# A two-layer relational graph network on one core: groups of 512 nodes summed in PSUM, bases over four chunks at once, no copied rows

## The chip, the cores and the metric

The kernel runs on one core of a Trainium2 chip. The metric is the device time of one execution in microseconds (us), lower is better. Times of the changed kernel are compared with those of the kernel before, run on the same chip.

## The reference: what is computed

There are N = 50,000 nodes with 128 features each and E = 850,000 edges, sorted by their destination. Each edge has a source, a destination and one of 16 relations. 50,000 of the edges are loops (one for each node, the last of its edges), so M = 800,000 others are left. A layer sums the sources' features per destination and relation and multiplies them by the matrix of the relation, which is itself a weighted sum of 8 bases. All is float32.

```python
def _rgcn_layer(h, src, dst, rel, basis, w_comp, loop_w, bias):
    W = jnp.einsum('rb,bio->rio', w_comp, basis)          # 16 x 128 x 128 from 8 bases
    seg = dst.astype(jnp.int32) * N_REL + rel.astype(jnp.int32)
    agg = jax.ops.segment_sum(h[src], seg, num_segments=N_ENT * N_REL)
    agg = agg.reshape(N_ENT, N_REL, -1)
    msg = jnp.einsum('nri,rio->no', agg, W)
    out = msg + h @ loop_w + bias
    return jax.nn.relu(out)
h = _rgcn_layer(x, src, dst, rel, basis1, w_comp1, loop_w1, bias1)
h = _rgcn_layer(h, src, dst, rel, basis2, w_comp2, loop_w2, bias2)
out = layernorm(x + h)
```

## The kernel before

**Chunks.** The 800,000 edges are cut into 6,250 tiles of 128 edges, and ten tiles (K) make a chunk: 625 chunks (C) in each of the two layers. For each tile, GpSimd (POOL) issues one indirect DMA (`gather`, L202), which fetches the 128 source rows of 512 bytes, in layer 1 from x and in layer 2 from H1, the first layer's output in HBM. The tiles go to five buffers `rows`, `g0` to `g4`, used in turn (GATHERS). In chunk c, POOL gathers the tiles of chunk c + 2 (L932 to L935). A gather waits until TensorE (PE) has used the tile that it overwrites, which is of chunk c - 3.

**From edges to slots.** A tile's edges end in at most 12 neighbouring nodes (WN), its slots. VectorE (DVE) writes a matrix `hot` (L871) of 128 edges by 8 bases by 12 slots: the weight that the edge's relation has for the base, at the edge's slot. PE multiplies the gathered tile by it (L964, 96 columns). Five tiles share a PSUM bank `pa`, two of which are used in turn, and ScalarE (ACT) copies each to `aT` in SBUF (L972). Two chunks later `slots` (L730 to L740) multiplies the 120 slots of the chunk by the 8 bases: 8 matmuls of 128 columns into one bank `ps` (L734), which ACT copies to `slots` (L739).

**From slots to nodes.** `masks_of` (L742) makes two matrices on DVE that say which node, of the 128 from the chunk's base on, a slot belongs to: one for the chunk's own slots and one for those of the chunk before. `nodes_of` (L757) multiplies them by the slots (L761) into `pn`, adds the loop part, and takes relu (layer 1) or adds x and normalizes (layer 2). Each chunk writes 128 rows, and neighbouring chunks' rows overlap.

**The loop part.** `from_itself` (L692) takes 128 nodes: a transpose (L209), two matmuls of 512 columns by four bases each (L710), a product with the node's weights (L713), the product with the loop matrix (L722, L723), and a sum over nine parts (L726). The result goes to L in HBM (L727) and is read again at the chunk's base (`loaded`, L879).

**Rows copied by hand.** In two of eight chunks the tenth tile isn't gathered by POOL. `row_by_row` (L789) lets a sequencer read the 128 source addresses into registers (L798) and issue 128 DMAs of one row each (L808): SP's for one of the two chunks and ACT's for the other. These instructions stand in the same queues as SP's other loads and as ACT's copies. There are 308 such tiles in the two layers, 154 on each of the two.

**Order.** The order on PE, POOL, DVE and ACT is the program's order (manual schedule, L853). `beside` (L901) puts the other parts' steps between the ten matmuls of a chunk. An engine works its queue in order; a waiting instruction holds those behind it. In the first layer, the lists of sources and slots for later chunks are made alongside, one step a chunk (`later_rows`, L839); ten times each a scatter to FULL (L378) and one to LREL (L434) stand among POOL's gathers.

Of the kernel before, what the change touches and what calls it, by code (L numbers as in the profile page):

```python
# [39 lines left out]
F32 = mybir.dt.float32  # L40
I32 = mybir.dt.int32
# [21 lines left out]
AHEAD = 4  # L63
# [8 lines left out]
BASES = 8  # L72
BY_HAND = 8
# [8 lines left out]
def tile_rgcn_resnorm(  # L82
# [21 lines left out]
    NG, NT = -(-R // P), -(-N // P)  # L104
# [9 lines left out]
    assert D == P and N >= P and edges.shape[0] == 1 and AT * NR == P and PER * NB * WN <= BANK and AT * PER * NB == WEIGHTS and PER == HALF and S <= P and C >= 4 and M > 0 and RUN - LK // 2 == LIVE and 2 * C <= NG * P and N <= 1 << 16 and E % ROW == 0  # L114
# [10 lines left out]
    ROW_AT = dram.tile([2 * C, P], I32, name="ROW_AT")  # L125
    NL = -(-(N + LK) // P) * P
    LREL = dram.tile([2 * NL, 1], I32, name="LREL")

    L = [dram.tile([N, D], F32, name=f"L{n}") for n in range(2)]
# [67 lines left out]
    ps_o = ctx.enter_context(tc.tile_pool(name="ps_o", bufs=1, space=PSUM))  # L197
    ps_n = ctx.enter_context(tc.tile_pool(name="ps_n", bufs=1, space=PSUM))
    ps_h = ctx.enter_context(tc.tile_pool(name="ps_h", bufs=2, space=PSUM))
# [6 lines left out]
    def turned(h, m, sb):  # L206

        tp = ps_o.tile([P, D], F32, name="po")
        nc.tensor.transpose(tp[:, :m], h, ident[:m, :m])  # L209
        hT = sb.tile([P, P], F32, name="hT")  # L210
        nc.scalar.copy(hT[:, :m], tp[:, :m])
        return hT[:, :m]
# [8 lines left out]
    key = consts.tile([P, 2 * C * HALF], BF16, name="key")  # L221


    base_i = consts.tile([1, C], I32, name="base_i")
    slot = consts.tile([P, C], F32, name="slot")
    next_slot = consts.tile([P, C], F32, name="next_slot")
    last_slot = consts.tile([P, 1], F32, name="last_slot")
    first_of = consts.tile([1, C], F32, name="first_of")
    base1 = consts.tile([1, C], F32, name="base1")
    minus = consts.tile([1, S], F32, name="minus")  # L230
# [4 lines left out]
    picked = consts.tile([P, 5 * NG + len(ROWS) + 4], F32, name="picked")  # L235
    ones = consts.tile([P, max(LIVE, C)], F32, name="ones")
# [10 lines left out]
    nc.vector.memset(minus, -1.0)  # L247
# [5 lines left out]
    def set_up(pool):  # L253
# [14 lines left out]
        po = ps_o.tile([P, D], F32, name="po")  # L268
# [146 lines left out]
    def loops_of(g, pool, m, d_i, k_f, r_i, loop, loops, asked):  # L415
# [15 lines left out]

        nc.vector.tensor_scalar(picked[0:1, 5 * g + 4 : 5 * g + 5], d_i[0:1, 0:1], float(asked()), None, op0=OP.is_ge)
        yield
# [8 lines left out]
    def rows_of(j, pool):  # L442
# [3 lines left out]
        parts = pool.tile([P, 2, LIVE, 2], F32, name="parts")  # L446
        for h in range(2):
            nc.sync.dma_start(
                parts[:m, h],
                FULL[h * NP + r0 * LIVE : h * NP + (r0 + m) * LIVE].rearrange("(p e) w -> p e w", e=LIVE),  # L450
            )
        if j:
            yield
        srcf = pool.tile([P, LIVE], F32, name="srcf")
        nc.vector.tensor_tensor(srcf[:m], parts[:m, 0, :, 0], parts[:m, 1, :, 0], op=OP.add)
        node = pool.tile([P, LIVE], I32, name="node")
        nc.vector.tensor_tensor(node[:m], parts[:m, 0, :, 1], parts[:m, 1, :, 1], op=OP.add)
# [20 lines left out]
        row_at = pool.tile([P, LIVE], F32, name="real").bitcast(I32)[:, :P]  # L478
        nc.vector.tensor_scalar(row_at[:m], srcf[:m, LIVE - P :], float(N - 1), float(4 * D), op0=OP.min, op1=OP.mult)
        nc.sync.dma_start(ROW_AT[r0 : r0 + m], row_at[:m])  # L480

# [3 lines left out]
        keyf = pool.tile([P, LIVE], F32, name="keyf")  # L485
# [6 lines left out]
        if (r0 + m) * LIVE > M:  # L492
# [6 lines left out]
                beyond[:m], place[:m, :LIVE], last[:m], 64.0, op0=OP.subtract, op1=OP.mult  # L499
# [8 lines left out]
        po = ps_o.tile([P, D], F32, name="po")  # L508
# [6 lines left out]
        nc.vector.tensor_scalar(base1[:, c0 : c0 + cs], half[0:1, :, 0], float(N - P), None, op0=OP.min)  # L515
        nc.vector.tensor_scalar(base_i[:, c0 : c0 + cs], base1[:, c0 : c0 + cs], float(4 * D), None, op0=OP.mult)

        a, b = max(c0 - 1, 0), c0 + cs - 1
        off = pool.tile([1, P], F32, name="off")
        nc.vector.tensor_tensor(off[:, : b - a], base1[:, a + 1 : b + 1], base1[:, a:b], op=OP.subtract)  # L520
        yield
        po = ps_o.tile([P, D], F32, name="po")
        for h in range(2):
            nc.tensor.matmul(po[:S, :cs], spread[h], half[:, :, h], start=h == 0, stop=False)
        nc.tensor.matmul(po[:S, :cs], minus, base1[:, c0 : c0 + cs], start=False, stop=True)
        nc.vector.tensor_scalar(slot[:S, c0 : c0 + cs], po[:S, :cs], within[:S], None, op0=OP.add)
        yield
        po = ps_o.tile([P, D], F32, name="po")
        nc.tensor.matmul(po[:, : b - a], ones[0:1, :P], off[:, : b - a], start=True, stop=True)
        nc.vector.tensor_tensor(next_slot[:S, a:b], slot[:S, a:b], po[:S, : b - a], op=OP.subtract)  # L530
        if b == C - 1:
            nc.vector.tensor_tensor(
                last_slot[:S], next_slot[:S, b - 2 : b - 1], po[:S, b - a - 1 : b - a], op=OP.subtract
            )
# [6 lines left out]
            ones[:m, :LIVE],  # L541
# [6 lines left out]
    def count_up(pool):  # L548
        last = 5 * NG + len(ROWS)
        off = pool.tile([1, C], F32, name="off_all")  # L550

        nc.vector.memset(off, float(N - 1))
        nc.vector.tensor_copy(off[:, : C - 1], first_of[:, 1:])
        nc.vector.tensor_tensor(off, off, base1, op=OP.subtract)
        nc.vector.scalar_tensor_tensor(
            off, off, float(P - 1), ones[0:1, :C], op0=OP.is_le, op1=OP.mult, accum_out=picked[0:1, last : last + 1]
        )

        in_time = pool.tile([1, C], F32, name="in_time")
        nc.gpsimd.iota(  # L560
            in_time,
            pattern=[[P * NT // C, C]],
            base=P * AHEAD - P,
# [3 lines left out]
        nc.vector.tensor_tensor(off, base1, in_time, op=OP.subtract)  # L567
        nc.vector.scalar_tensor_tensor(
            off, off, 0.0, ones[0:1, :C], op0=OP.is_le, op1=OP.mult, accum_out=picked[0:1, last + 1 : last + 2]
        )  # L570

        nc.vector.tensor_tensor(off[:, : C - 3], base1[:, 2 : C - 1], first_of[:, 1 : C - 2], op=OP.subtract)
        nc.vector.tensor_tensor(off[:, C - 3 : C - 2], base1[:, C - 1 :], first_of[:, C - 3 : C - 2], op=OP.subtract)
        nc.vector.scalar_tensor_tensor(
            off[:, : C - 2],
            off[:, : C - 2],
            1.0,
            ones[0:1, : C - 2],
            op0=OP.is_ge,
            op1=OP.mult,  # L580
            accum_out=picked[0:1, last + 3 : last + 4],
        )
        nc.vector.tensor_scalar(picked[0:1, last + 2 : last + 3], first_of[:, 0:1], 0.0, None, op0=OP.is_equal)
# [3 lines left out]
        total = ps_o.tile([P, D], F32, name="po")  # L587
# [4 lines left out]
            off[:, 1:2], total[:1, 1:2], float(E + 2 * NG * (P + 1) + 3 * C - 1), None, op0=OP.not_equal  # L592
# [3 lines left out]
    def normed(t, m, sb):  # L596

        *_, o = normed_steps(t, m, sb)
        return o

    def normed_steps(t, m, sb):
        st = sb.tile([P, 6], F32, name="st")
        nc.vector.bn_stats(st[:m], t)  # L603
        mv = sb.tile([P, 2], F32, name="mv")
        nc.vector.bn_aggr(mv[:m], st[:m])
        sd = sb.tile([P, 1], F32, name="sd")
        nc.scalar.activation(sd[:m], mv[:m, 1:2], AF.Sqrt, bias=eps[:m])  # L607
        yield
        rs = sb.tile([P, 1], F32, name="rs")
        nc.vector.reciprocal(rs[:m], sd[:m])  # L610
        nm = sb.tile([P, 1], F32, name="nm")
        nc.vector.scalar_tensor_tensor(nm[:m], mv[:m, 0:1], -1.0, rs[:m], op0=OP.mult, op1=OP.mult)
        o = sb.tile([P, D], F32, name="o")
        nc.scalar.activation(o[:m], t, AF.Identity, bias=nm[:m], scale=rs[:m])  # L614
        yield o

    def chunked():
        with (
# [8 lines left out]
            def at(c):  # L627

                if c % BASES == 0:
                    _, starts[:] = nc.values_load_multi_w_load_instructions(  # L630
                        base_i[0:1, c : min(C, c + BASES)],
                        engines=[mybir.EngineType.SP],
                        min_val=0,
                        max_val=(N - P) * 4 * D,
                        skip_runtime_bounds_check_because="bases are clamped to N - P, and no node is below 0",
                    )
                return starts[c % BASES]

            def nodes_at(of, start):
                return of.bitcast(U8).rearrange("n d -> (n d)")[ds(start, P * 4 * D)].rearrange("(p d) -> p d", p=P)  # L640

            def weights(c, n):
# [14 lines left out]
                for j in range(PER):  # L657
# [6 lines left out]
                    )  # L664
                yield pm.rearrange("e (t b) -> e t b", b=NB)

            def loop_weights(i, n):

                m = min(AT, NT - i) * NR
                rel = hp.tile([P, 2, P], I32, name="lrel")  # L670
# [536 lines left out]
```

## Time and profile before

| | |
|---|---|
| median of 3 runs | 19472.55 us (19454.4 to 19488.24) |
| the profiled execution | 19472.55 us, its span 19470.8 us |
| PE | 11516.4 us busy, 59% |
| POOL | 11559.5 us busy, 59% |
| DVE | 6757.1 us busy, 35% |
| ACT | 2523.1 us busy, 13% |
| TensorE clock granted, mean | 0.722 |
| DMA engines | 2 tenths busy, 63 GB/s |
| first gather of layer 1, of layer 2 | at 46.52 us, at 9864.63 us |

The span is divided by two layers of 625 chunks, so a chunk takes about 15.6 us. No engine is busy for more than 59% of the span: what sets the time must be read from what each engine waits for. In the profile's groups, a float32 matmul is two records, so that 24,384 records of L964 are 12,192 matmuls. "Busy" is the union of an engine's records. "issue" as the end of a wait means that the profile shows nothing that was waited for.

### The profile page before, as it was taken

What the parts mean: (1) busy time and instruction counts of PE and PEld (TensorE: products, weight loads), DVE (VectorE), ACT (ScalarE), POOL (GpSimd) and SP (SyncE); (2) the same over time, 40 slices, a digit from 0 to 9 for tenths busy, and PEclk for the clock granted to TensorE, in tenths of its full rate; (3) what the DMA queues carried; (4) which work ended last, traced back from release to release, by engine and by line L of the source; (5) the groups of instructions that cost most, each with busy time, mean ns of one, the idle gap of its engine ahead of it and who ended that gap; (6) DMA issues with size and microseconds to landing.
All of it is one profiled execution on the core that took longest, in us unless ns stands there. A gap on an engine that the chain in (4) does not pass through costs nothing. (4 is left out here: it accounts for less than half of the span.)

```text
span 19470.8 us, 266458 instructions
## 1 busy us (share of the span) xinstructions
PE 11516.4 (59%) x59202; PEld 9701.4 (50%) x59202; DVE 6757.1 (35%) x14585; ACT 2523.1 (13%) x6567; POOL 11559.5 (59%) x12224
## 2 busy tenths in 40 slices
PE   4555555555566665566655556556656565666666
PEld 3444444454455555555545545445545555555555
DVE  4333333333322232223233333333333333333333
ACT  0111111111111111111111111111111111111111
POOL 5555555555566666666655656556556566666565
PEclk7677777767677777777767777776777777777767
DMA  2222222222222222222222222222222222222222
GB/s 73 63 67 66 63 62 64 62 68 63 62 61 62 61 61 61 61 61 61 60 57 64 63 64 64 64 63 65 63 64 64 64 65 64 65 64 64 64 64 60
DMA packets 1236553, 1233.00 MB, mean 63 GB/s; under 512 B 318005, under 2 KB 1028333, under 8 KB 1234941
## 3 DMA queue, kind: packets, MB, share of 16 engines
q0 software_dynamic: 393696, 806.61, 15.9%
q1 hardware_dynamic: 798604, 397.62, 7.1%
q10 hardware_dynamic: 42640, 11.62, 0.3%
q8 instruction: 481, 7.88, 0.2%
q14 instruction: 1132, 9.27, 0.2%
HBM read 1059.71 MB, written 154.87 MB: 62 GB/s over the span
## 5 line engine op out<-in xcount | busy, mean ns | idle before, releaser
L964 PE MATMUL pa<-hot,g 128*128 128x96 f32 x24384 | 5507.6, 336 | 4909.6 <-issue 3201.8
L964 PEld LDWEIGHTS pa<-hot,g 128*128 128x128 f32 x24384 | 4948.1, 256 | 6503.9 <-issue 4657.1
L202 POOL DMA_INDIRECT g<-H,src x6096 | 5762.1, 945 | 3840.1 <-PE pa L964 1495.0
L202 POOL DMA_INDIRECT g<-in_x_dram,src x6096 | 5771.5, 947 | 3559.5 <-issue 1401.8
L734 PE MATMUL ps<-basis,aT 128*120 128x128 f32 x20000 | 4165.3, 343 | 264.9 <-issue 245.7
L734 PEld LDWEIGHTS ps<-basis,aT 128*120 128x120 f32 x20000 | 3525.2, 245 | 292.7 <-issue 271.5
L972 ACT COPY aT<-pa 128x480 f32<-128x480 f32 x2500 | 1397.9, 559 | 9783.0 <-DMA by_hand<-in_x_dram 2847.3
L710 PE MATMUL hb<-basis,hT 128*128 128x512 f32 x3128 | 2411.4, 862 | 59.6 <-issue 52.9
L713 DVE TENSOR_TENSOR by<-hb,lw 128x512 f32<-128x512 f32 x1564 | 1075.4, 688 | 3632.9 <-PE pa L964 941.1
L723 DVE TENSOR_TENSOR by<-po,bias 128x128 f32<-128x128 f32 (+1 forms) x782 | 227.6, 291 | 4532.3 <-PE pa L964 2156.7
L726 DVE TENSOR_REDUCE ls<-by 128x128 f32<-128x1152 f32 (+1 forms) x782 | 1649.2, 2109 | 13.6
L871 DVE TENSOR_TENSOR hot<-fixed,own 128x960 f32<-128x960 f32 x1250 | 1447.1, 1158 | 92.5 <-remote 19.8
L761 PE MATMUL pn<-slots,own 120*128 120x128 f32 x5000 | 1065.4, 343 | 396.6 <-issue 225.5
L209 PE MATMUL po<-ident,h_own 128*128 128x128 f32 (+1 forms) x782 | 297.1, 380 | 1537.3 <-ACT lw L689 841.4
L761 PEld LDWEIGHTS pn<-slots,own 120*128 120x128 f32 x5000 | 885.3, 246 | 441.8 <-issue 260.6
L209 PEld LDWEIGHTS po<-ident,h_own 128*128 128x128 f32 (+1 forms) x782 | 157.7, 202 | 1621.4 <-ACT lw L689 855.2
L864 DVE TENSOR_TENSOR own<-fixed,key 128x120 f32<-128x120 f32 x1250 | 343.3, 275 | 1346.5 <-PE pa L964 542.0
L610 DVE RECIPROCAL rs<-sd 128x1 f32<-128x1 f32 x625 | 100.1, 160 | 1856.3 <-issue 1129.7
L710 PEld LDWEIGHTS hb<-basis,hT 128*128 128x128 f32 x3128 | 669.4, 263 | 76.5 <-issue 67.4
L722 PE MATMUL po<-loop,hT 128*128 128x128 f32 x1564 | 399.8, 344 | 419.5 <-issue 210.6
L658 PE MATMUL fixed<-each,is_rel 128*128 128x64 f32 x3140 | 529.1, 326 | 97.5 <-issue 96.2
L658 PEld LDWEIGHTS fixed<-each,is_rel 128*128 128x128 f32 x3140 | 512.6, 247 | 98.8 <-issue 97.3
(152 smaller groups left out, 4602.8 us busy)
## 6 DMA issues: line engine op xcount, KB each, us to landing
by_hand<-in_x_dram ACTq DMA_DIRECT2D x9856, 0.5 KB
by_hand<-in_x_dram SPq DMA_DIRECT2D x9856, 0.5 KB
by_hand<-H ACTq DMA_DIRECT2D x9856, 0.5 KB
by_hand<-H SPq DMA_DIRECT2D x9856, 0.5 KB
g<-in_x_dram,src POOLq DMA_INDIRECT x6096
g<-H,src POOLq DMA_INDIRECT x6096
ls_of<-L SPq DMA_DIRECT2D x1250, 64.0 KB
L<-ls SPq DMA_DIRECT2D x780, 64.0 KB
```

Source lines behind the costliest of these rows:

```text
L202: return nc.gpsimd.indirect_dma_start(out=to, out_offset=None, in_=of, in_offset=bass.IndirectOffsetOnAxis(ap=idx, axis=0))
L209: nc.tensor.transpose(tp[:, :m], h, ident[:m, :m])
L658: nc.tensor.matmul(of[:, :, j * NB : (j + 1) * NB], is_rel[:m, j * P : (j + 1) * P], EACH[n][:m], start=True, stop=True,)
L710: nc.tensor.matmul(hb[:m], hT, BASIS[n][:, b : b + few, :].rearrange("p b d -> p (b d)"), start=True, stop=True)
L713: nc.vector.tensor_tensor(by[:m, b : b + few, :], hb[:m].rearrange("p (b d) -> p b d", d=D), lw[:m, b : b + few, None].to_broadcast([m, fe ...
L722: nc.tensor.matmul(po[:m], hT, LOOP[n], start=True, stop=True)
L726: nc.vector.tensor_reduce(ls[:m], by[:m].rearrange("p b d -> p d b"), AX.X, OP.add)
L734: nc.tensor.matmul(ps[: k * WN], aT[:, b, : k * WN], BASIS[n][:, b, :], start=b == 0, stop=b == NB - 1)
L761: nc.tensor.matmul(pn, own, st[i][: ks(i) * WN], start=j == 0, stop=j == len(masks) - 1)
L871: nc.vector.tensor_tensor(hot[:, : ks(c)], pm[:, c % Q * K : c % Q * K + ks(c), :, None].to_broadcast([P, ks(c), NB, WN]), own[:, : ks(c), ...
L964: nc.tensor.matmul(pa[:, i * NB * WN : (i + 1) * NB * WN], g[:, k + i, :] if k + i < ks(c) - by_hand(c) else handed.pop(c), hot[:, k + i]. ...
L972: nc.scalar.copy(aT[:, :, k * WN : (k + m) * WN].rearrange("d b (i w) -> d i b w", w=WN), pa[:, : m * NB * WN].rearrange("d (i b w) -> d i ...
```

## The change

1. **No copied rows.** `row_by_row`, its address table and its place in the chunk loop are gone. POOL gathers all ten tiles of each chunk.
2. **Bases over four chunks.** `aT` holds four chunks (480 slots). One matmul for each base multiplies them all (`slots_of_batch`, after's L746: 8 matmuls of 480 columns for four chunks), with the base as the stationary side, so the result stands by features and has to be turned back: a copy by ACT (`by_slot`), four transposes (L756), and a DVE product per chunk (`spread_out`, L734) which places each slot's row in one of four columns by the node's number modulo 4. The last chunks go one by one (`slots`).
3. **Groups of 512 nodes.** 98 groups with 4 nodes in each partition. Each chunk's slots are multiplied by one mask for each group that the chunk can touch (L788, 512 columns) and are added up in the group's PSUM bank `pn`. A chunk starts 80 nodes after the one before if the edges are spread evenly; the kernel takes a margin of 128 nodes on both sides, and a test at the end runs the slow general path if a chunk lies further off. The loop matrix's product goes to the same bank (L798); the rest of the loop part stays in SBUF (`ls`) instead of going through L. `finish` adds, takes relu or normalizes, and writes 512 rows at once.
4. Lists in narrower types (`key` in 8 bits, `own` in BF16), and fewer working tiles.

Each gather waits, as before, for the product that read its own tile.

The core of the diff:

```diff
-    ps_o = ctx.enter_context(tc.tile_pool(name="ps_o", bufs=1, space=PSUM))
-    ps_n = ctx.enter_context(tc.tile_pool(name="ps_n", bufs=1, space=PSUM))
-    ps_h = ctx.enter_context(tc.tile_pool(name="ps_h", bufs=2, space=PSUM))
+    ps_o = ctx.enter_context(tc.tile_pool(name="ps_o", bufs=2, space=PSUM))
+    ps_s = ctx.enter_context(tc.tile_pool(name="ps_s", bufs=1, space=PSUM))
+    ps_n = ctx.enter_context(tc.tile_pool(name="ps_n", bufs=2, space=PSUM))
...
+            def spread_out(c, of):
+                k = ks(c) * WN
+                st = sb.tile([P, J, D], F32, name="slots", bufs=BATCH)
+                nc.vector.tensor_tensor(
+                    st[:k],
+                    of[:k, None, :].to_broadcast([k, J, D]),
+                    which[:k, c, :, None].to_broadcast([k, J, D]),
+                    op=OP.mult,
+                )
+                return st
+
+            def slots_of_batch(c, aT, st, n):
+                ps = ps_s.tile([P, BANK], F32, name="ps")
+                for b in range(NB):
+                    nc.tensor.matmul(
+                        ps[:, : BATCH * S], BASIS[n][:, b, :], aT[:, b, :], start=b == 0, stop=b == NB - 1
+                    )
+                    if b < NB - 1:
+                        yield
+                by_slot = sb.tile([P, BATCH * S], F32, name="by_slot", bufs=1)
+                nc.scalar.copy(by_slot, ps[:, : BATCH * S])
+                yield
+                po = ps_o.tile([P, BANK], F32, name="po")
+                for q in range(BATCH):
+                    nc.tensor.transpose(po[:S, q * P : (q + 1) * P], by_slot[:, q * S : (q + 1) * S], ident)
...
+            def to_nodes(c, n):
...
+                    nc.tensor.matmul(
+                        sums[g],
+                        own,
+                        of[:k].rearrange("s j d -> s (j d)"),
+                        start=c == first(g),
+                        stop=c == final(g),
+                    )
+                    if c == first(g):
+                        hT = hTs.pop(g)
+                        for j in range(J):
+                            nc.tensor.matmul(
+                                sums[g][:m, j * D : (j + 1) * D], hT[:, j, :m], LOOP[n], start=False, stop=False
+                            )
...
+            def finish(g, n):
+                m = nodes(g)
+                ls = lss.pop(g)[:m]
+                nc.vector.tensor_tensor(ls, sums.pop(g)[:m].rearrange("p (j d) -> p j d", j=J), ls, op=OP.add)
+                if n == 0:
+                    yield
+                    nc.scalar.activation(ls, ls, AF.Relu)
+                    nc.sync.dma_start(of_group(H1, g), ls)
...
-            def row_by_row(engine, c, of):
...
-                        for k in range(ks(to) - by_hand(to)):
+                        for k in range(ks(to)):
                             gather(rows[buffer][:, k, :], of, src[:, to * K + k : to * K + k + 1])
-                    for engine, at_chunk in HANDS:
-                        if by_hand(c + BY_HAND + 1) and (c + BY_HAND + 1) % BY_HAND == at_chunk:
-                            fetching[at_chunk] = row_by_row(engine, c + BY_HAND + 1, of)
-                            handed[c + BY_HAND + 1] = next(fetching[at_chunk])
...
-                    aT = aTs[c] = hp.tile([P, NB, S], F32, name="aT", bufs=3)
+                    if c % BATCH == 0:
+                        aTs[c // BATCH] = hp.tile([P, NB, BATCH * S], F32, name="aT")
```

Counted in the built programs, the two layers issue: 12,500 gathers (12,192 before); on PE 12,500 products with `hot` (12,500 before), 2,480 base products of 480 columns and 80 of 128 (10,000 of 128 before), 2,064 node products of 512 columns (2,500 of 128), 1,568 of 512 columns in the loop part (1,564), 2,024 transposes (782), 784 loop products (782) and 1,570 for the weights (1,570).

## Prediction

> **What bounds the kernel now.** I read the groups first, then the waits, then POOL's timeline, then two windows.
>
> The groups show that no engine works through: a chunk takes 15.6 us (19470.8 / 1250), POOL's gathers in it 9.2 us (11533.6 / 1250) and PE's records 9.2 us (11516.4 / 1250).
>
> ```profile
> L964 PE MATMUL pa<-hot,g 128*128 128x96 f32 x24384 | 5507.6, 336 | 4909.6 <-issue 3201.8
> L202 POOL DMA_INDIRECT g<-H,src x6096 | 5762.1, 945 | 3840.1 <-PE pa L964 1495.0
> L972 ACT COPY aT<-pa 128x480 f32<-128x480 f32 x2500 | 1397.9, 559 | 9783.0 <-DMA by_hand<-in_x_dram 2847.3
> ```
>
> The last number of a line is what ended the idle time: POOL waits for PE's products, PE for nothing visible and for ACT's copy of `aT`, and ACT, which is 13% busy, sat idle for 9783.0 us before that copy. Its waits say for what:
>
> ```profile
> ACT aT L972 <- DMA by_hand<-in_x_dram: 2847.3, 569, 46.3
> PEld pa L964 <- ACT aT L972: 1782.6, 579, 20.4
> ACT sd L607 <- DMA by_hand<-H: 1512.3, 329, 14.7
> ACT aT L972 <- DMA by_hand<-H: 1487.0, 629, 8.1
> ACT o L768 <- DMA by_hand<-in_x_dram: 1068.5, 418, 17.5
> ACT o L614 <- DMA by_hand<-H: 943.1, 379, 8.0
> ```
>
> The five waits of ACT for `by_hand` add up to 7858.2 us. A copied tile is 128 DMA issues and 8 address loads in ACT's queue (L808, median 228 ns; L798, median 1298 ns): 128 x 0.228 + 8 x 1.298 = 39.6 us at the least, and the copies of `aT` stand behind them. So the chain is: rows copied on ACT, late `aT`, PE without a `pa` bank, POOL without a free tile.
>
> What POOL does when nothing holds it, the timeline shows (start, duration, and in brackets the idle time before):
>
> ```profile
> 5050.51 0.94 POOL L202 DMA_INDIRECT g<-in_x_dram,src  x1 [0.30 <-issue]
> 5051.76 0.94 POOL L202 DMA_INDIRECT g<-in_x_dram,src  x1 [0.30 <-DMA g<-in_x_dram,src]
> 5053.01 0.94 POOL L202 DMA_INDIRECT g<-in_x_dram,src  x1 [0.30 <-issue]
> 5054.25 0.94 POOL L202 DMA_INDIRECT g<-in_x_dram,src  x1 [0.30 <-issue]
> ```
>
> One gather in 1.248 us: from 5038.01 to 5076.72 there are 31 steps, 38.71 / 31 = 1.249, and from 9864.63 to 9935.80 there are 57, 71.17 / 57 = 1.249. That is 12.48 us a chunk, the floor for a kernel that gathers all ten tiles.
>
> **The change part by part.**
>
> *No copied rows.* POOL gets 308 gathers more: 308 x 1.248 = +384 us of its own time. It had 12,192 x 1.248 = 15,216 us of work in 19,470.8, so this is paid out of its waiting. ACT and SP lose 39,424 row DMAs, and the 7858 us of ACT's waits have no cause left. What is late next is POOL itself, at 12,500 x 1.248 = 15,600 us. Bounds: if only ACT's `aT` waits named above go (4334 us), the span falls to 15,136, below POOL's floor; if PE finds other waits, nothing goes.
>
> *Bases over four chunks.* On PE 10,000 matmuls (L734) go; 2,480 of 480 columns and 1,240 transposes come. Nearest row is L710 with 512 columns: two records take 1.05 us at full clock (12050.58) and 1.97 at half (12045.11), times 480/512: 0.98 and 1.85. ACT: 310 copies of 480 columns at 0.559 (L972) = 173 us for 338.3 (L739). DVE: 1,250 products of 512 out of PSUM at 0.688 (L713) = +860 us.
>
> *Groups of 512.* On PE 2,500 matmuls of 128 columns become 2,064 of 512 at 1.05 to 1.97. DVE has 2,064 masks for 2,500 at 0.303 (-132 us), no L723 (-228), and 196 sums at 0.688 for 1,250 at 0.281 (-216); normalizing keeps its work per row of features. With the 860 that makes about 7,040 us for 6757, 45% of 15,800. The trip through L (782 writes, 1,250 loads) was on SP, off the path.
>
> *PE's sum.* At full clock, from the stretch 19428 to 19435: 12,500 x 0.258 (8 records in 1.03) + 2,480 x 0.98 + 2,064 x 1.05 + 1,568 x 1.05 + 2,024 transposes x 0.33 (L209) + 784 x 0.41 (L722) + 1,570 x 0.25 (L658) + some 100 for the loop weights = 10,950 us, 8.8 us a chunk. At half clock the same terms are 0.505 (8 records in 2.02 at 9815.70), 1.85, 1.97, 1.97, 0.42 (L209's median), 0.82 (twice), 0.48 (10 records in 2.39 at 9834.55) and 190: 20,490 us, 16.4 a chunk. POOL's 12.48 lies between the two. PE keeps up while the granted clock is above 0.68 (work done per us is w / 10,950 + (1 - w) / 20,490, which reaches 1 / 15,600 at w = 0.36, and the clock is 0.5 + 0.5 w). It was 0.722 over the span. The windows tell which way it goes:
>
> ```profile
> core 0: us, PE busy (x) PEld busy (x) DVE busy (x) ACT busy (x) POOL busy (x), PEclk, DMA share, GB/s
> 9865.00:9950.00 85.00, 24.36 (x58) 14.44 (x58) 5.81 (x8) 2.98 (x7) 64.28 (x69) 0.51 0.22 58
> 19428.00:19435.00 7.00, 7.00 (x64) 6.91 (x64) 1.39 (x6) 3.58 (x9) 0.00 (x0) 1.00 0.09 25
> ```
>
> In the first PE is 29% busy at clock 0.51, in the second all busy at 1.00. A PE that falls behind at half clock becomes all busy and gets the full one, at which it does a chunk in 8.8 us; and POOL may run three chunks (37 us) ahead before it feels PE's lag. So I take PE as hidden behind POOL. If that cover is gone, its price is the second rival's.
>
> *Waits.* The gather's two waits stay as they are. New ones are PE's for the two `po` banks that DVE empties (L709, 0.688; the sum L717, 2.109, stands before the next). Per column of nodes 0.688 x 2 + 2.109 = 3.5 us of DVE, 784 times, 2.7 ms; queued behind such a wait on PE are products whose tiles are in SBUF already. Bounds: 0 (while POOL is late anyway) and +2.7 ms on PE's sum, 10.95 + 2.7 = 13.7 ms, still below 15.6 at full clock. I take 0. The 20 scatters between the gathers stay. POOL's idle time before them was 458.5 us (L378 273.5, L434 185.0), because POOL ran ahead of DVE. If POOL is last it comes two chunks after DVE; bounds 0 and 458; I take 45, a tenth, and 15 for the first, at 99.23, which stands right at the start.
>
> *A rule of the skill.* In this trace one copied tile costs ACT at least 39.6 us of its queue, a gathered one costs POOL 1.248. The Trainium skill, DMA: Bandwidth & Descriptors, Issuing engine by pattern, says the opposite in general, that the hardware queues (SP, ACT) are the faster ones and GpSimd's path the more flexible; by it, moving 308 tiles to POOL would only add its 384 us. It speaks of one transfer; here a single issue serves 128 rows.
>
> *The sum.* To the first gather 46.5 (before's row); 12,500 x 1.248 = 15,600; 20 scatters x 1.5 (1.17 + 0.30) = 30; start and scatter waits 15 + 45; between the layers 30 and after the last gather 30. For these two, before shows 48.6 (the wait for H1) and 52.7 (19417.2 + 0.94 to 19470.8), with PE up to three chunks behind; the instructions alone (two copies, 8 base products, `spread_out`, two node products, add, relu, store) are some 10. Together 15,796.5, and 1.75 around the span (19472.55 - 19470.8; this execution is the median): **15,800 us**, -18.9%.
>
> **The rivals.**
>
> 1. *PE and POOL go on trading waits*, in groups instead of rows. For it: at before's mean rows (busy over matmuls, as 5507.6 / 12,192 = 0.452) PE would need 12,500 x 0.452 + 2,480 x 1.445 + 2,064 x 1.54 + 1,568 x 1.54 + 2,024 x 0.38 + 784 x 0.51 + 1,570 x 0.337 + 150 = 16,700 us, more than POOL. Against: those rows hold half-clock time of a PE that was idle 41% of the span. Price: 16,700 + 150 for both ends = 16,850.
> 2. *PE stays at half clock* (slower than before). Place: the ten products of a chunk, each released by a gather every 1.248 us, so that PE idles in between, as in the first window above. Price: 20,490 + 150 = 20,640 us. It decides from a granted clock below 0.53 (w = 0.06 gives 19,470). Against: at that clock PE has 16.4 us of work in 12.5 and can't idle. The Trainium skill, TensorE: Matmul & The Clock Gate, Part 1, has the same two rates and a window of about 3.4 us for either switch; the two windows agree with the rates (0.51, 1.00), and by it both this rival's idle gaps and the cure are possible.
> 3. *The change doesn't do what it says*: a chunk's start lies over 128 nodes off the even spread, and the general path runs after all. In the reference's inputs the starts lie -22 to +58 nodes off. Price: far over before.
>
> **How the numbers follow.** Forecast, POOL's floor with both ends (15,700 to 16,100): 0.75. Rival 1, 16,100 to 17,000: 0.15; worse mixtures of it up to before's time: 0.05. Rival 2: 0.03, rival 3: 0.01, within 0.2% (39 us, about what a measurement of this kernel can tell from no change): 0.01. The low end is 46.5 + 15,600 + 30 with 10 for each end and nothing else, 15,700; the high end takes in rival 1, 16,900. That leaves out about 0.1. Faster 0.95, same 0.01, slower 0.04.
>
> **What would show it.** Right: POOL busy about 75% (0.945 / 1.248) in all 40 slices; gathers' idle time nearly all "issue" at 0.30; 12,500 gathers in two stretches of about 7,800 us; PE waiting for the gathers' DMAs; no ACT wait for a row's DMA. Wrong: gathers released by PE for more than some 200 us (rival 1), a granted clock below 0.68 with PE over 90% busy (rivals 1 and 2), or gathers longer than 0.95 us, since nothing else shortens 12,500 steps.

## The result, and the profile after

The changed kernel takes 18,461.54 us (median of 4, 18,435.78 to 18,465.47), the kernel before beside it 19,463.47 us (4 runs): 0.9482 of the time, 95% interval 0.9466 to 0.9499. The forecast was 15,800 us. The direction came true, the size did not: 1,002 us went, not 3,670. The two kernels don't take the same time on every chip, so each experiment is compared with the kernel before on its own chip, and that one took 15,410 to 15,441 us on two chips and 19,460 to 19,780 us on the others, the result's among them.

The groups of the page that answer to those of before:

```profile
L202 POOL DMA_INDIRECT g<-H,src x6250 | 5929.8, 949 | 3090.0 <-issue 1304.3
L202 POOL DMA_INDIRECT g<-in_x_dram,src x6250 | 5938.3, 950 | 3029.0 <-issue 1267.5
L974 PE MATMUL pa<-hot,g 128*128 128x96 f32 x25000 | 4581.9, 308 | 3009.5 <-issue 2081.6
L982 ACT COPY aT<-pa 128x480 f32<-128x480 f32 x2500 | 1388.0, 558 | 15113.3 <-remote 8194.1
```

A gather takes 0.95 us as before, but the 12,500 of them now stand idle for 6119 us in all where 0.30 each would be 3750. ACT waits longer for the banks than before, 15,113 us for 9783, though no copied row is left in its queue. The list of waits says for whom (total us, times, longest us):

```profile
ACT aT L982 <- remote: 8194.1, 813, 47.8
PEld pa L974 <- issue: 5010.2, 10168, 31.5
ACT aT L982 <- PE pa L974: 4464.2, 1043, 17.2
POOL g L202 <- remote: 1822.6, 1379, 6.1
DVE by L709 <- remote: 1469.1, 246, 57.9
```

"Remote" means an update of the awaited semaphore whose sender the profile doesn't find: no instruction that sends it ended close before it. The semaphore here is PE's. The same word stood in the list of waits of before, for 5,400 us in all, and the prediction passed over it:

```profile
ACT aT L972 <- remote: 1904.5, 316, 30.5
DVE by L723 <- remote: 1292.7, 167, 46.3
```

One stretch of the timeline of after shows what such a wait is:

```profile
12006.88 0.36 PE L974 MATMUL pa<-hot,g 128*128 128x96 f32 x2
...
12008.08 0.56 ACT L982 COPY aT<-pa 128x480 f32<-128x480 f32 x1 [8.72 <-PE ps L746]
...
12011.30 0.36 PE L974 MATMUL pa<-hot,g 128*128 128x96 f32 x2
...
12015.81 0.56 ACT L982 COPY aT<-pa 128x480 f32<-128x480 f32 x1 [7.17 <-remote]
12015.81 1.16 DVE L876 TENSOR_TENSOR hot<-fixed,own 128x960 f32<-128x960 f32 x1 [13.47 <-remote]
12016.04 0.95 POOL L202 DMA_INDIRECT g<-H,src  x1 [1.33 <-remote]
12016.42 0.53 PE L974 MATMUL pa<-hot,g 128*128 128x96 f32 x1 [4.76 <-issue]
```

PE is done with all that it may do at 12,011.7 and then idle for 4.76 us. Its next product needs the bank that ACT copies at 12,015.81. That bank's fifth product, the first line, had ended at 12,007.2; ACT was idle from 12,008.6 on and could have copied it then. At 12,015.8 to 12,016.0 ACT, DVE and POOL start together, just after an update of PE's semaphore at 12,015.78; all three wait for that semaphore. The granted clock follows, so that the windows lie between the two that the prediction showed:

```profile
core 0: us, PE busy (x) PEld busy (x) DVE busy (x) ACT busy (x) POOL busy (x), PEclk, DMA share, GB/s
9000.00:9100.00 100.00, 61.87 (x231) 40.73 (x230) 33.00 (x48) 9.30 (x17) 65.88 (x70) 0.73 0.19 52
18375.00:18430.00 55.00, 43.34 (x240) 30.05 (x238) 29.97 (x73) 11.56 (x26) 1.00 (x2) 0.92 0.06 18
```

PE isn't waiting for gathers: a product starts 63 us after its gather in the median, within 3 us of it in 0.16% of cases. POOL is 44 tiles ahead of PE in the median, of 50 possible. So in this run the late hand-overs between PE, ACT and DVE set the pace, 14.7 us a chunk (18,434 / 1250), and POOL waits for freed tiles. (By themselves, without gathers, the three take 8.1 us a chunk: l3 below.)

How late PE's signals are can be counted in every trace, from the end of a bank's fifth product to the start of ACT's copy, and from the updates themselves:

| kernel, run | us | bank's end to ACT's copy, median us | PE's updates seen within 60 ns of the end | ACT's updates in the record |
|---|---|---|---|---|
| before, the prediction's | 19,472.55 | 8.91 | 20% | 2530 of 6566 |
| after, the result's | 18,435.78 | 3.19 (mean 5.15) | 28% | 1579 of 3411 |
| after, other chip (a1) | 15,831 | 0.04 | 99.9% | 3411 of 3411 |
| after, late chip (l1) | 18,460 | 2.79 | 29% | 1639 of 3411 |
| before without rows, late chip (l2) | 18,613 | 6.36 | 16% | 3650 of 6566 |
| before without rows, other chip (e4) | 15,785 | 0.04 | 99.8% | 6560 of 6566 |

Where signals are late, many events are also missing from the record (of PE's own updates 16,377 of 19,684 are there in the result's trace), so the fourth column is too low there. The third doesn't depend on it, but in the kernel before it also holds the time of ACT's row issues: with twice the rows it is 13.9 us on a chip where updates are on time (b4), so 8.91 is not to be read as lateness alone. In the trace of before the lateness begins with the first gather, at 46.5 us, and ends with the last, at 19,417: from 19,424 on every update is seen within 15 ns, as it is in the gap of 49 us between the two layers' gathers (9820 to 9864).

### The profile page after: what moved, and what is told of

The parts are those of the page before. It is cut to its first block, busy times and chain, and to the rows that moved or that the text cites. A ratio compares the mean times of both kernels' runs of the same rounds, so it can differ in the third digit from the quotient of the medians.

```text
span 18434.0 us, 136664 instructions
## 1 busy us (share of the span) xinstructions
PE 11416.0 (62%) x45072; PEld 7482.7 (41%) x45072; DVE 6704.1 (36%) x11496; ACT 1926.2 (10%) x3706; POOL 11894.1 (65%) x12533
## 5 line engine op out<-in xcount | busy, mean ns | idle before, releaser
L974 PEld LDWEIGHTS pa<-hot,g 128*128 128x128 f32 x25000 | 4547.2, 229 | 6044.9 <-issue 5010.2
L974 PE MATMUL pa<-hot,g 128*128 128x96 f32 x25000 | 4581.9, 308 | 3009.5 <-issue 2081.6
L746 PE MATMUL ps<-aT,basis 128*128 128x480 f32 x4960 | 2910.5, 672 | 707.7 <-ACT aT L982 476.2
L788 PE MATMUL pn<-slots,own 120*128 120x512 f32 x4128 | 2553.4, 741 | 615.4 <-DVE slots L734 289.2
L702 PE MATMUL po<-basis,hT 128*128 128x512 f32 x3136 | 2048.6, 741 | 1319.1 <-DVE by L709 1101.2
L709 DVE TENSOR_TENSOR by<-po,lw 128x512 f32<-128x512 f32 x1568 | 1069.5, 687 | 4167.5 <-remote 1469.1
L734 DVE TENSOR_TENSOR slots<-po,which 120x512 f32<-120x512 f32 x1240 | 782.6, 683 | 2747.6 <-remote 933.8
L788 PEld LDWEIGHTS pn<-slots,own 120*128 120x128 f32 x4128 | 865.5, 238 | 1202.2 <-issue 687.4
L746 PEld LDWEIGHTS ps<-aT,basis 128*128 128x128 f32 x4960 | 879.1, 221 | 754.3 <-ACT aT L982 494.9
L702 PEld LDWEIGHTS po<-basis,hT 128*128 128x128 f32 x3136 | 563.8, 225 | 1390.6 <-DVE by L709 1151.7
L756 PE MATMUL po<-ident,by_slot 128*120 128x128 f32 x1240 | 317.9, 348 | 1129.2 <-ACT by_slot L752 742.8
L756 PEld LDWEIGHTS po<-ident,by_slot 128*120 128x120 f32 x1240 | 178.3, 181 | 1171.5 <-ACT by_slot L752 770.4
L771 DVE TENSOR_SCALAR own<-col,node 120x128 f32<-120x128 f32 x2064 | 529.4, 296 | 10.4 <-PE pn L788 10.4
L798 PEld LDWEIGHTS pn<-loop,hT 128*128 128x128 f32 x1568 | 234.5, 213 | 134.0 <-issue 133.6
```

The costliest lines, as they stand in the source:

```text
L702: nc.tensor.matmul(hb[:m], hT[:, j, :m], BASIS[n][:, b : b + few, :].rearrange("p b d -> p (b d)"), start=True, stop=True,)
L709: nc.vector.tensor_tensor(by[:m, b : b + few, :], hb[:m].rearrange("p (b d) -> p b d", d=D), lw[:m, j, g % T, b : b + few, None].to_broadc ...
L734: nc.vector.tensor_tensor(st[:k], of[:k, None, :].to_broadcast([k, J, D]), which[:k, c, :, None].to_broadcast([k, J, D]), op=OP.mult,)
L746: nc.tensor.matmul(ps[:, : BATCH * S], BASIS[n][:, b, :], aT[:, b, :], start=b == 0, stop=b == NB - 1)
L771: nc.vector.tensor_scalar(own[:k], col4[:k], node4[:k, c : c + 1], float(-g * GN), op0=OP.subtract, op1=OP.is_equal)
L788: nc.tensor.matmul(sums[g], own, of[:k].rearrange("s j d -> s (j d)"), start=c == first(g), stop=c == final(g),)
```

## The experiments

"On time" and "late" say which kind of chip a run fell on: chips 14 and 11 (two groups of runs) were on time, chips 15 (two groups) and 1 late. With six groups on four chips, that it is the chip and not what else went on there is likely, not shown. The runs of e1, e2, f1 to f5, l3 and l4 are single ones; the differences that they are read for are 1% (f4) and 6% (f5) or far larger, or none within 1%.

**Gathers taken away, gathers set free, four buffers, one part alone (e1 to e4, on time).**

```diff
# e1_no_gathers, later l3
-                        for k in range(ks(to)):
+                        for k in range(ks(to) if to < GATHERS else 0):
# e2_apart, later l4
-                        buffer = (n * C + to) % GATHERS
+                        buffer = (n * C + to) % (GATHERS - 1)
...
+                            if n == to == 0:
+                                gather(rows[GATHERS - 1][:, k, :], of, src[:, k : k + 1])
-                    g = rows[(n * C + c) % GATHERS]
+                    g = rows[GATHERS - 1]
# e3_four_buffers
-GATHERS = 5
+GATHERS = 4
# e4_no_rows, later l2 (on the kernel before)
-            HANDS = ((nc.sync, BY_HAND - 1), (nc.scalar, BY_HAND // 2 - 1))
+            HANDS = ()
```

> The changed kernel, in which only the first five chunks of each layer are gathered (100 gathers); every later product reads the tiles that are there, so the sums are of other rows. PE, DVE, ACT and SP do what they did. If POOL and PE trade waits (rival 1) or the gathers are the floor, the time falls to PE's own work at full clock, 11,000 to 12,500 us. If the 14.7 us of a chunk are set by PE, ACT and DVE among themselves, it stays within 3% of 18,434 us. If gathers that run beside PE slow the signal from PE to ACT and DVE, it falls as well, and the time from the end of a bank's fifth product to the copy of that bank (median 3.2 us, 75% point 8.5 us in the changed kernel) falls to under 0.1 us.

> The changed kernel, in which all gathers go to four of the five buffers and all products read the fifth, filled once (12,510 gathers), so the sums are of other rows: POOL waits for no product and no product waits for a gather. Floor theory: the gathers end at 46 + 12,510 x 1.248 + the scatters = 15,700 us, and PE ends with or before them, span 15,700. PE, ACT and DVE theory: the gathers end at 15,700 and the products go on to some 18,000 to 18,500. Slowing by the gathers: as the last one, but the pace of a chunk drops from 14.7 us towards 9 us as soon as the gathers have ended, so 17,000 to 18,000.

> The changed kernel with four buffers of ten tiles in place of five. POOL may run 40 tiles ahead of PE, not 50. If POOL and PE trade waits, the smaller lead costs: 2 to 8% slower. If PE never waits for a gather (in the changed kernel a product starts 66 us after its gather in the median, within 3 us of it in 0.2% of cases), nothing changes: within 1%.

> One part alone: the kernel before with no copied rows, all ten tiles gathered, rows per 128 nodes and bases per chunk as they were. By the prediction's step, the 7858 us of ACT's waits go and POOL's floor is next: 15,700 to 17,000 us. If PE, ACT and DVE set the pace among themselves, the row waits only lay beside other waits: 18,400 to 19,500, and the change's 5% come from fewer and wider instructions.

Measured beside 15,410 us: e1 10,059 us, e2 15,790, e3 15,801 (1.0254 [1.0236, 1.0271]), e4 15,785 (1.0242 [1.0225, 1.0259]). e2, e3 and e4 agree with the floor theory, and e3 with a changed kernel at 15,831 us (a1). e1 falls below the 11,000 to 12,500 us that it foresaw for PE's own work, a sum that was too high. The kernel before itself takes 4,000 us less here than in the prediction's profile, so that these four can't say why the result was late. They say that the floor theory holds on another kind of chip.

**The changed kernel there, and the copied tiles doubled (on time).** The second is the kernel before with `BY_HAND = 4`.

> The changed kernel itself, beside the kernel before. In the four runs with this change's result PE's signals came late (in the trace a third of PE's updates are seen within 60 ns of the instruction's end, against all of them in the run with four buffers). If that lateness is what made the forecast fail, then on a chip on which the signals are on time this kernel takes 15,790 us (46 + 12,500 x 1.248 + both ends), 2.4% more than the 15,410 us that the kernel before took in the last runs; where they are late it takes 18,460 us, 5% less than the 19,460 us of the kernel before. If instead the change itself holds POOL up, it takes over 16,500 us where the kernel before takes 15,410.

> The kernel before with twice the copied tiles (one tile of a chunk in two, 616 in place of 308; 11,884 gathers). Floor theory, signals on time: each copied tile takes 1.248 us off POOL and nothing else is late, 15,410 - 308 x 1.248 = 15,025 us. If ACT's waits for rows set the pace (the step that the prediction began with), the copies of the intermediate results come later and it takes 15,500 to 16,500 us. With late signals: 19,500 to 20,500 us.

a1: 15,831 us, 1.0252 [1.0238, 1.0266] of the kernel before (15,441). The forecast of 15,800 is met within 0.2%, and on such a chip the change is a loss: 390 us, where 308 gathers x 1.248 make 384 (the rows alone, e4, cost 375). Its groups:

```profile
L974 PE MATMUL pa<-hot,g 128*128 128x96 f32 x25000 | 5662.0, 327 | 3163.7 <-DMA g<-in_x_dram,src 1524.1
...
L202 POOL DMA_INDIRECT g<-in_x_dram,src x6250 | 5954.8, 953 | 1936.3 <-issue 1131.5
L202 POOL DMA_INDIRECT g<-H,src x6250 | 5933.6, 949 | 1922.8 <-issue 1200.2
L982 ACT COPY aT<-pa 128x480 f32<-128x480 f32 x2500 | 1396.3, 559 | 12762.8 <-PE pa L974 12750.5
```

PE now waits for gathers, and POOL's idle time is 3859 us, 0.31 a gather. b4 takes 24,825 us (1.608 [1.605, 1.610]), not 15,025: on time, 308 copied tiles lengthen nothing and 616 are the bound (ACT waited 7,900 and 2,901 us for them before copies of `aT`). The expectation was missed: ACT's waits for rows do set the pace, but only at twice the number.

**A late bank made by hand, and many small loads (on time).** In f1 and f2 the copy of `aT` stands in a loop of six (`for _ in range(COPIES)`), in the changed kernel and in the one before; f3 adds four 4-byte loads on SP in each step of `beside`.

> The changed kernel, in which ACT makes each copy of aT six times to the same place (2,500 x 5 x 0.56 = 7.0 ms of ACT, which was 10% busy), so that PE gets a bank of products back 2.8 us later, as if the signal of PE had come 2.8 us late (in the four runs with this change's result the copy started 3.2 us after the bank's fifth product in the median, 5.1 in the mean). If late banks are what takes POOL off its floor there, PE falls behind and the time rises from 15,830 to 17,500 to 19,500 us, with POOL's gathers released by PE for over 1,000 us. If a lateness of that size is covered by POOL's lead and PE's slack, it stays at 15,830 within 1%, and the lateness of the other signals (to DVE, to by_slot, to POOL) must have done it.

> The same six copies in the kernel before, whose ACT also issues the copied rows. Late banks theory: 18,500 to 20,500 us, more than the changed kernel with the same six copies, since here ACT's row issues (39.6 us a tile) stand in the same queue. If the lateness is covered: 15,440 within 1%.

> The changed kernel with 40 loads of 4 bytes more per chunk on SP's queue (50,000 in all) into small tiles that nothing reads: almost no bytes, but 16 semaphore updates each, some 50 per us beside the 15 per us of the gathers and the rest. If updates from DMAs crowd out PE's (in the four runs with this change's result PE's came late only from the first gather to the last), PE's updates come late here too: under 90% of them within 60 ns of the end, and the time rises by over 2%. If it is a matter of the chip or of how its events are taken down, nothing changes: within 1% of 15,830 us, unless SP itself becomes late.

Measured beside 15,414 us: f1 15,802, f2 18,946, f3 15,901. A bank given back a constant 2.8 us late costs the changed kernel nothing and the kernel before 23%. So the two differ there, but that doesn't explain the late chips: there the changed kernel is slow too. f3 doesn't either: 100,000 DMA updates more in the record (21.7 per us in all, for 15.5), and 99.6% of PE's still on time. The loads brought two updates each, not the 16 expected, so more crowding than that wasn't tried.

**Late hand-overs on a late chip, and copied tiles in the changed kernel.** These runs fell on a late chip (the kernel before: 19,723 us). f4 is e4 with the six copies; f5 is f1 with each product of L709 made five times; r2 is the changed kernel with `row_by_row` put back on SP and ACT, `BY_HAND = 4` and four buffers.

> The kernel before without copied rows (one part of the change alone), with the six copies of aT. With the copied rows the six copies took 18,946 us, in the changed kernel 15,802. If it is the rows in ACT's queue that make the kernel before give way to a late bank, this one stays at POOL's floor, 15,790 us within 1%. If it is the rest of the old structure (bases per chunk and rows per 128 nodes), it takes over 17,000 us.

> The changed kernel with the six copies of aT and, in DVE, each product out of po (196 x 8 = 1,568) made five times to the same place, so that PE also gets the two po banks back 2.75 us later each (DVE: 1,568 x 4 x 0.688 = 4.3 ms more). The prediction bounded the waits for po at 0 to 2.7 ms and took 0. If these two late hand-overs together are what took POOL off its floor in the four runs with this change's result, 17,000 to 19,500 us; if they too are covered while POOL is late anyway, 15,800 us within 1%.

> The changed kernel with copied tiles put back, twice as many as the kernel before had (616; 11,884 gathers), and four buffers of ten tiles to make room. Since a late aT cost the changed kernel nothing, ACT's row issues should not either: floor theory 15,830 - 616 x 1.248 = 15,060 us, 2.4% less than the kernel before. If rows late in ACT's and SP's queues set the pace as in the kernel before with twice the rows, over 18,000 us.

f4 19,029 us, 0.965 of the kernel before; f5 19,820 us, 1.005; r2 24,664 us, 1.2515 [1.2495, 1.2536]. The numbers expected were for the other kind of chip, so f4 and f5 don't answer their questions: on top of late signals, the bank's delay costs f4 some 1% (0.956 without it, l2), and delays of bank and `po` together cost f5 6% (0.948 without, l1). r2's question has an answer, with the late signals beside it: at 616 tiles the rows set the pace, here too.

```profile
POOL g L204 <- PE pa L1014: 9229.0, 3489, 17.6
ACT aT L1022 <- DMA by_hand<-in_x_dram: 9161.5, 1048, 26.0
ACT aT L1022 <- DMA by_hand<-H: 8890.7, 1018, 48.3
```

**The four decisive ones, on one late chip.**

> The changed kernel once more, to have it on the same chip as the next three. Where PE's signals are late (the kernel before over 19,000 us): 18,400 to 18,800 us, 5% less than the kernel before. Where they are on time: 15,830 us, 2.5% more.

> One part alone again (the kernel before without copied rows). On a chip with late signals: if the gain of 5% is that of the removed rows (the prediction's first step, ACT's 7858 us of waits), 18,400 to 18,800 us like the changed kernel; if it is that of fewer signals from PE (22,303 updates of its semaphore before, 19,684 after) and of wider work, it stays at 19,300 to 19,700 us. On time: 15,790 to 15,820 us.

> The changed kernel with only the first five chunks of a layer gathered, again (later products read other rows than the reference's). On a chip with late signals: if the gathers beside PE are what makes PE's signals late, they are on time here and it takes 10,060 us as on the other chip; if the chip delays PE's signals by itself, over 13,000 us with most of PE's updates later than 60 ns. On time: 10,060 us.

> Gathers and products apart, again (products read tiles filled once, so the sums are of other rows). On a chip with late signals: if PE, DVE and ACT by themselves set the pace there and POOL only waits for them, the gathers end at 15,700 us and the products go on to 17,500 to 18,500 us; if POOL and PE trade waits, both end at about 15,790 us. On time: 15,790 us.

Beside 19,463.5 us: l1 18,460 us, 0.9483 [0.9467, 0.9500], the result again. l2 18,613, 0.9561 [0.9545, 0.9577]: taking away the copied rows alone brings 4.4 of the 5.2%, all the rest 0.8%. l3 10,112 us, as on the other chip, with 99.5% of PE's updates on time: **no gathers, no lateness**. l4 25,909 us, far beyond what any theory expected: with gathers that wait for nothing the kernel is 40% slower than with gathers that wait (l1). Windows of l4, during and after the second layer's gathers:

```profile
14000.00:15000.00 1000.00, 131.10 (x352) 82.25 (x352) 62.88 (x105) 18.31 (x35) 769.07 (x715) 0.53 0.17 49
23000.00:24000.00 1000.00, 949.89 (x4575) 637.02 (x4575) 639.59 (x1103) 204.82 (x411) 0.00 (x0) 0.96 0.06 20
```

And the same kernel where signals are on time (e2):

```profile
9000.00:10000.00 1000.00, 945.38 (x4523) 634.99 (x4522) 640.03 (x1104) 203.64 (x410) 756.84 (x799) 0.96 0.25 73
```

Columns are PE, PEld, DVE, ACT, POOL, clock, DMA share, GB/s. Beside 715 gathers in 1000 us PE does 352 matmul records on the late chip, and 4,523 beside 799 on the other. What ACT waited for in l4:

```profile
ACT aT L984 <- remote: 14308.6, 330, 68.8
```

So on such a chip running gathers hold up the signals of PE. It isn't that l4 makes more gathers per time: 715 in 1000 us there, 70 in 100 us in the result's window, in which PE did 231 records. What l4 lacks is the breaks. The result's own trace has them: of PE's ends with four gathers begun in the 5 us before, 16% have an update within 60 ns; with two 54%; with none 99%. While a gather runs and up to 1 us after it, it is 25%; from 4 us after the last gather on it is 96% or more (a1: over 99% throughout). This fits a balance in the changed kernel, which no run tried by itself: PE starves while POOL gathers, POOL then runs out of freed tiles and waits, and in that time the signals get through.

**Pauses between gathers (late, the kernel before 19,777 us).** After every fifth (p1) or tenth (p2) gather POOL makes an iota that nothing reads.

```diff
                             gather(rows[buffer][:, k, :], of, src[:, to * K + k : to * K + k + 1])
+                            if k % 5 == 5 - 1:
+                                nc.gpsimd.iota(pause, pattern=[[1, 448]], ...)
```

> The changed kernel, in which POOL makes an iota of 448 elements (about 0.47 us by L246's 691 ns for 672, with its overhead some 0.6) after every fifth gather: 2,500 pauses. If on a chip with late signals it is the gathers back to back that hold the signals up, and a pause lets them through, more of PE's updates are seen within 60 ns (28% in the changed kernel there) and the time falls below 18,460, at best to 15,830 + 2,500 x 0.6 = 17,300 us; if the pauses are too short or the gathers' number alone decides, 18,460 to 19,500 us. Where the signals are on time POOL is the floor and each pause costs: 17,000 to 17,400 us.

> The same with a pause after every tenth gather: 1,250 pauses. With late signals that pauses let through: between the changed kernel and the one with twice the pauses, 17,000 to 18,200 us; if pauses don't matter, 18,460 to 19,000 us. On time: 16,400 to 16,650 us.

p1 18,671 us, 0.9443 [0.9426, 0.9460]; p2 18,688, 0.9454 [0.9437, 0.9470]. The changed kernel wasn't run on this chip; against its 0.9483 elsewhere that is at best 0.4% less. PE's updates within 60 ns stay at 28 and 29%. So pauses of 0.53 us don't let the signals through, and the hoped-for 17,300 is missed; the result's trace has them on time only after some 4 us without a gather, and no pause of that length was tried. But p1's pauses put 1327 us on POOL (2,500 x 0.531) and didn't lengthen the run: they came out of POOL's waiting (5004 us before gathers, for 6119). POOL's own time isn't the bound there.

## Why the prediction was wrong, by its own steps

**The step that failed** is "the 7858 us of ACT's waits have no cause left. What is late next is POOL itself", with "So I take PE as hidden behind POOL". On a late chip that removal alone gave 850 us (l2) of the 3,670 forecast, and ACT's idle time before `aT` was still 11,439 us:

```profile
L972 ACT COPY aT<-pa 128x480 f32<-128x480 f32 x2500 | 1390.7, 556 | 11438.5 <-remote 5745.1
```

The cause that was left is PE's late signal, so the wait that was priced by its last releaser had a second one under it. A wait for several semaphores is put down to the one that came last; in before that was often a row's DMA, and with the rows gone PE's signal is the last. The trace of before held the sign on an engine without rows: DVE's product L713 started over 1 us after both the end of its matmul (L710) and the end of DVE's own last instruction in 440 of 1,564 cases (in e4, on time, in none). The prediction read who ended the waits, and never whether PE's end agreed with when its waiters went on. The Trainium skill, Perfetto Trace Analysis, Per-engine timelines, says that TensorE's end in a profile is an estimate and that the update goes out only when PSUM has acknowledged the data; where signals are on time the end and the update lie 14 ns apart here (median, a1); where they are late it is microseconds (8.5 in the stretch above).

**No copied rows: +384 us on POOL.** Right where POOL is the bound (375 for the rows alone, 390 for the whole change), and then it is the whole effect. Where signals are late it is covered, and removing the rows pays.

**Bases over four chunks, groups of 512.** DVE was put at 7,040 us and took 6,704; PE's sum at full clock at 10,950, and e1 shows 9,396 busy in 10,059 at clock 0.957. Both were too high (the stretch named for PE's sum holds no row of L209 or L722), and neither was on the path. Together these parts are worth nothing on time (1.0252 with them, 1.0242 without) and 0.8% where signals are late.

**PE keeps up above a clock of 0.68.** On time it does (0.83, PE 79% busy). In the result the clock was 0.762, above the limit, and PE was late all the same: the limit holds for a PE that always has work it may do, and this one waited for updates.

**Waits for `po`, taken as 0.** On time 7.2 us before L702's matmuls in a1. In the result 1,101 us (258 times), so there the term is not nothing.

**Scatters 15 + 45 and the ends.** On time POOL stood 36 us before them (L375 31.1, L430 4.7); in the result 363, near the upper bound of 458. To the first gather 46.3 (46.5 foretold), between the layers 18 in a1 (30), after the last gather 24 (30).

**The rule on queues.** The Trainium skill, DMA: Bandwidth & Descriptors, Issuing engine by pattern, has the hardware queues as generally the faster ones. No run here shows it for a single row. 128 issues for what POOL does in one gained 375 us at 308 tiles on time (e4) and lost wherever there were 616 (b4 24,825 us, r2 24,664).

**The rivals.** Rival 1 had the right picture, PE and POOL trading waits, but at 16,850 us: its price came from PE's rows, not from PE's signals. Rivals 2 and 3 did not occur. The signs the prediction asked for said so plainly: POOL 65% busy and not 75, gathers released by PE for 1,139 us and by unknown senders, in fact PE's updates, for 1,823, where "more than some 200" was to mean rival 1. In a1 the signs of being right are there: POOL 75%, two stretches of some 7,900 us, PE waiting for gathers. The sign of 200 us can't stand as written, though: a1 has 635 us under that name too, in waits of at most 0.3 us each, where the result has waits of up to 5.8.

The range, 15,700 to 16,900, lay where a chip with signals on time puts the changed kernel. That is no success in part: on such a chip the 3,670 us to be saved aren't there, and the change loses 2.5%. That the direction came true is luck as far as the forecast goes, since it hangs on late signals that the forecast didn't know of. That the profile of before might belong to a chip with a further limit wasn't among the cases.

**What stays open:** why some chips hold PE's signals up while gathers run. Shown is that the gathers are needed for it (l3) and that gathers without breaks make it worse (l4). Not told apart is what of a gather does it: POOL's issuing, the rows' bytes or the 16 updates that each one brings. In those runs events are missing from the record as well, and whether taking the record is itself what is slow there wasn't tried: every time here is that of a recorded execution. How the removal of rows brings 4.4% on such a chip isn't shown either: the bank's mean wait goes from 9.1 us to 6.6 and, with the rest of the change, 5.1, but the first of these also holds ACT's row issues.

No version that beats both kernels was found: on time the kernel before is the fastest of all that were run whole, where signals are late the changed kernel (or the one with pauses).

## What to carry to other kernels

Before pricing a wait by who ended it, check that the producer's end and the waiter's start agree: here one subtraction on the profile of before (matmul done, DVE idle, product started over 1 us later in 440 of 1,564 cases) would have told that PE's results were late to an engine that issues no rows, and so would the 5,400 us of waits whose sender wasn't found, which no run on time has. A floor read from the unhindered stretches of one engine holds only if the rest can run beside that stretch for long; the time that an engine spends waiting may be what lets the others go on. And a change that trades one engine's work for another's can change sign with the chip: 5% faster here, 2.5% slower there.

## What the hardware showed unexpectedly

- On a late chip gathers that wait for nothing slow down themselves as well: in l4 6,786 of 12,509 steps lie between 1.38 and 1.42 us (in e2, on time, 40; the median there is 1.249). The longer gaps between PE's updates in the result's trace cluster at 0.7, 1.4, 2.1 and 2.8 us, multiples of some 0.70.
- A bank copied 2.8 us late costs nothing in one kernel (f1, 15,802) and 3,500 us in the other (f2, 18,946), which also issues 308 tiles' rows and has bases and sums the old way; which of these makes it give way was not told apart on time.
- Where signals are on time, four buffers of ten tiles do as well as five (1.0254 and 1.0252), so that 5 KB of SBUF per partition are free. Late, that wasn't tried alone.
